# An attention kernel on one core: each output projection's seven products put into one run, its reads due first, and all dates of the build-time planner replaced

## The chip, the cores and the metric

The kernel runs on one core of a Trainium2 chip. The metric is the time of one execution in device microseconds; the median of three runs of the kernel before is 1901.77 us (1901.64 to 1901.78). Names of engines: PE is TensorE's matmuls and PEld its loads of weights, DVE is VectorE, ACT ScalarE, POOL GpSimd, SP the queue of SyncE that issues most transfers.

## The reference

A cross-attention layer with a residual, followed by a linear state-space scan over the same rows and a few small outputs. Cut to the attention, which is nearly all of the work (T = 4096 queries, S2 = 3202 keys, H = 512, 8 heads of 64, fp32):

```python
q, k, v = heads(q_in, Wq, bq), heads(kv_in, Wk, bk), heads(kv_in, Wv, bv)
scores = einsum('bhqd,bhkd->bhqk', q, k) / sqrt(HD)
out = einsum('bhqk,bhkd->bhqd', softmax(scores), v)
x1 = x + out @ W_o.T + b_o          # then the scan, state by state, over the rows of x1
```

q_in and kv_in are layer-normed rows of x and of the context.

## The kernel before

**Stages.** A lead (to 196 us) normalises the context and makes keys and values. The main loop (196.1 to 1846.3 us) goes over 8 blocks Q of 512 queries, in each over 4 pairs of heads and 2 halves of the queries: 64 units. A unit has 13 chunks of keys, and for each chunk: a score group s on TensorE (L1133, 16 records of 64x64 tiles in the trace), its exponential p on ScalarE (L1211), the product with the values po on TensorE (L1269, 16 records), and the addition of p to a running sum acc on VectorE (L1219). The last chunk is a half one. At a unit's end acc is folded (L1226), swapped and gathered (L1238, L1243), summed by a matmul pd (L1298), inverted (L1342 and L1347), joined (L1320 and L1324) and scaled (L1358). A tail (1846.3 us to the end) finishes the last block's output projection (yb, L2076), the state-space scan (a chain of small steps z over PE, ACT and DVE, L1924 to L1966), its products py and pd_last (L1998) and the joins of the rows (L2012 to L2018), and a short chain of its own for the last rows (zl, py_o1, xr_l: L2115 to L2225).

**Two modes of the array.** Score and value products use TensorE as four tiles of 64x64 (in the planner "quarters"); projections use the full 128x128 array. Here an interruption means a stretch of full-array work inside the stream of quarters.

**Projections by seven products.** A block's queries and its outputs are projected as 2x2 blocks with seven products in place of eight. `project_by_sevenths` makes the output projection of the blocks 0 to 6 (block 7 has `project`). Its pieces: `load` and `row` bring the rows of x and add the bias (SP and POOL); four sums `so` on VectorE ("5": a21 + a22 into a spare tile, "6": that minus a11, "7": a11 - a21 in place, "3": a12 minus sum 6); seven products in the order of CHAIN, 1 2 6 5 7 3 4, of eight records and 128x256 each; and after each one a read on VectorE that adds the accumulator to x1. The weights of the products are W_o or sums of its parts (`to`, made by POOL at L1508). Two accumulators alternate: pax for 1, 6, 7, 4, pay for 2, 5, 3. Products 1 and 2 add to nothing before them; 6 follows 1 in pax once read 1 is done, 5 follows 2 in pay after read 2, 7 after read 6, 3 after read 5, 4 after read 7. Sum 5 waits for product 1, since the tiles of o that the sums use are taken up by `open_left`, which product 1 calls; so the sums cannot be made ahead of the first product.

**Who sets the order.** All instructions are ordered at build time by the class `Plan`, a list scheduler: each piece has an engine, a cost, the pieces it waits for, rings of buffers it takes and gives, and a due date. At each step an engine takes the ready piece that fits and has the earliest due date. SHIFT adds to the due date of each sort of piece a number of steps (one step is about one chunk). A full-array piece gets a date earlier by KEEP while the array is already full, and later by ALONE if no other full-array piece is ready; ENTER and LEAVE are planning costs of a change of mode. `PORT` lists VectorE's pieces that the planner does not put beside GpSimd's. The resulting order of each engine is fixed in the program; at run time the semaphores decide when each instruction starts.

The seven products get their place by this (`at` is the place in CHAIN):

```python
plan.add((*key, k), "PE", 1740, partial(product_, k), after + last_scale,
         d + STEP * 3 // 4 + at - (plan.ALONE if at > 1 else 0),
         ["m", "m"] if k == "1" else [], gives[k])
plan.add(("outs.read", Q, k), "DVE", 690, partial(read, k), [(*key, k)], d + at,
```

The functions that the change touches:

## Time and profile before

| what | us |
| --- | --- |
| median of 3 runs | 1901.77 (1901.64 to 1901.78) |
| the profiled execution, and its span | 1901.72, 1899.8 |
| lead / main loop / tail | 0 to 196.0 / 196.0 to 1846.3 / 1846.3 to 1899.8 |
| busy PE, DVE, ACT, POOL | 1884.8, 1545.2, 1178.1, 253.5 |
| granted clock of TensorE | 0.998 |

The 1.9 us between the profiled execution and its span lie ahead of the first and behind the last instruction. The page's chain of the work that ended last is empty for this trace, so the reading goes by the busy time of stretches, by the groups of instructions and by the timeline: its rows give start, duration, engine, line, operation, out<-in, tile, shape and count, and in brackets the idle time before and who ended it. The ends of matmuls are modelled: their pace is to be taken from start to start. A busy TensorE in the main loop does not mean that it loses nothing: what a change of mode costs lies inside the busy time. Block 0's output projection starts at 430.54 us and block 1's at 637.62; the queries of block 2 are projected at 546.16.

### The profile page before, as it was taken

The numbers are of one execution on the slowest core, as the hardware profiler recorded it, in microseconds if no ns is written. First come the engines' busy times: TensorE is split into PE (matmuls) and PEld (weight loads), VectorE is DVE, ScalarE is ACT, GpSimd is POOL, SyncE is SP. The second block draws the span as 40 slices with busy tenths as digits, with TensorE's granted clock in tenths as the row PEclk, the third lists the DMA queues.
The fourth block names the chain that finished last, engine by engine and source line by source line (L and its number), as shares of the span: only waits on it lengthen the run. The fifth ranks groups of instructions, "written<-read, shape, count | busy, mean of one in ns | idle before, by whom it ended". The sixth has DMA issues, their size and how long they took to land.

```text
span 1899.8 us, 68757 instructions
## 1 busy us (share of the span) xinstructions
PE 1884.8 (99%) x29632; PEld 1383.5 (73%) x29632; DVE 1545.2 (81%) x2114; ACT 1178.1 (62%) x1677; POOL 253.5 (13%) x386
## 2 busy tenths in 40 slices
PE   9999999999999999999999999999999999999997
PEld 5887678777777777777777777777777777777684
DVE  6642699788978898799978897889969997988776
ACT  3242677575767567666766576657766675657653
POOL 6120300022000310022002200021002200120105
PEclk9999999999999999999999999999999999999999
DMA  8654233133323343223413332324312331536476
GB/s 254 159 158 118 59 103 91 41 112 91 97 74 105 92 110 89 77 76 105 112 43 113 83 110 78 105 78 113 101 55 89 112 104 44 171 111 177 136 200 225
DMA packets 260768, 207.55 MB, mean 109 GB/s; under 512 B 94632, under 2 KB 233896, under 8 KB 260460
## 3 DMA queue, kind: packets, MB, share of 16 engines
q1 hardware_dynamic: 256440, 196.48, 36.3%
q10 hardware_dynamic: 4020, 6.62, 1.2%
q8 instruction: 235, 3.85, 0.9%
q14 instruction: 73, 0.60, 0.1%
HBM read 156.32 MB, written 29.88 MB: 98 GB/s over the span
## 4 chain that ended last, share of the span: by engine, by line


## 5 line engine op out<-in xcount | busy, mean ns | idle before, releaser
L1211 ACT ACTIVATE p<-s,shifts 128x1024 f32<-128x1024 f32 (+1 forms) x832 | 895.0, 1082 | 458.1 <-PE s L1133 441.4
L1219 DVE TENSOR_TENSOR acc<-p,acc 128x1024 f32<-128x1024 f32 (+1 forms) x704 | 838.1, 1191 | 107.8 <-ACT p L1211 82.9
L1269 PE MATMUL po<-p,v 64*64 64x256 f32 x12800 | 849.5, 377 | 0.9 <-DVE o L1324 0.9
L1133 PE MATMUL s<-q,k 64*64 64x256 f32 x12800 | 850.1, 377 | 0.3 <-ACT p L1211 0.2
L1133 PEld LDWEIGHTS s<-q,k 64*64 64x64 f32 x12800 | 505.0, 133 | 197.2 <-ACT p L1211 12.9
L1269 PEld LDWEIGHTS po<-p,v 64*64 64x64 f32 x12800 | 504.0, 133 | 172.1 <-issue 6.9
L1622 POOL TENSOR_TENSOR xr<-xr,rowb 128x512 f32<-128x512 f32 x28 | 35.4, 1275 | 842.5 <-DVE acc L1219 842.5
L1347 DVE RECIPROCAL rd<-rd 128x256 f32<-128x256 f32 (+1 forms) x64 | 110.1, 1720 | 9.7 <-ACT rd L1342 9.7
L1219 DVE TENSOR_TENSOR acc<-p,p 128x1024 f32<-128x1024 f32 x64 | 78.1, 1220 | 26.5 <-ACT p L1211 26.4
L1713 POOL TENSOR_TENSOR xr<-x,modb 128x512 f32<-128x512 f32 x28 | 35.5, 1277 | 197.5 <-DVE acc L1219 155.5
L1243 DVE TENSOR_TENSOR acc<-swap,acc 64x256 f32<-64x256 f32 x126 | 56.1, 446 | 1.8 <-ACT swap L1238 0.2
L1204 DVE TENSOR_TENSOR acc<-x,acc 2x256 f32<-2x256 f32 x128 | 54.9, 429 | 1.4
L1409 POOL TENSOR_SCALAR rstd_x<-mv_x 128x1 f32<-128x1 f32 x28 | 18.9, 677 | 269.7 <-DVE mv_x L1406 268.0
L1559 ACT ACTIVATE q<-qx,bias 128x256 f32<-128x256 f32 x42 | 17.6, 471 | 56.8 <-PE qx L393 56.8
L1238 ACT COPY swap<-acc 64x256 f32<-64x256 f32 x126 | 50.9, 404 | 3.0
L571 DVE TENSOR_TENSOR ks<-pky,ks 128x512 f32<-128x512 f32 x15 | 10.4, 692 | 42.9 <-PE pky L393 28.1
L565 ACT ACTIVATE ks<-pkx,bias 128x256 f32<-128x256 f32 x40 | 16.8, 471 | 42.7 <-PE pkx L393 31.2
L1226 DVE TENSOR_TENSOR acc<-acc 128x512 f32<-128x512 f32 x63 | 42.9, 682 | 0.4
L1324 DVE TENSOR_TENSOR o<-po,o 128x256 f32<-128x256 f32 x64 | 26.9, 421 | 8.8 <-ACT o L1320 8.7
L1342 ACT ACTIVATE rd<-pd 128x128 f32<-128x128 f32 x126 | 33.6, 276 | 0.1
L1417 ACT ACTIVATE xh_y<-x,nm_y,rstd_y 128x512 f32<-128x512 f32 x30 | 24.3, 808 | 13.1 <-POOL nm_y L1411 13.1
L1167 DVE TENSOR_REDUCE m<-sm 128x1 f32<-128x256 f32 x64 | 23.8, 413 | 10.1 <-PE sm L1153 10.1
(312 smaller groups left out, 1754.2 us busy)
## 6 DMA issues: line engine op xcount, KB each, us to landing
k<-kd SPq DMA_DIRECT2D x432, 128.0 KB, 2.3
v<-vd SPq DMA_DIRECT2D x432, 128.0 KB, 2.3
xn<-x SPq DMA_DIRECT2D x448, 32.0 KB, 1.9
xr<-in_x_dram SPq DMA_DIRECT2D x30, 256.0 KB, 3.8
x1d<-xr SPq DMA_DIRECT2D x30, 256.0 KB, 2.8
x<-in_x_dram SPq DMA_DIRECT2D x28, 256.0 KB, 3.0
cx<-in_ctx_dram SPq DMA_DIRECT2D x25, 256.0 KB, 5.0
kd<-ks SPq DMA_DIRECT2D x20, 256.0 KB, 2.3
```

The costliest lines, as they stand in the source:

```text
L1133: nc.tensor.matmul(s[k0 : k0 + HD, a, b, :], kts[(*w["at"][:2], c)][r, b * CK + k0 : b * CK + k0 + HD], q[r], start=True, stop=True, skip_ ...
L1204: made = nc.vector.tensor_tensor(to[r], t[r], to[r], ALU.add)
L1211: nc.scalar.activation(t[:, :, :nb, :], w["ps"][c][:, :, :nb, :], AF.Exp, bias=w["shift"])
L1219: return nc.vector.tensor_tensor(w["acc"][:, :, :nb, :], t[:, :, :nb, :], before[:, :, :nb, :], ALU.add)
L1226: return nc.vector.tensor_tensor(acc[:, :, 0, :], acc[:, :, 0, :], acc[:, :, 1, :], ALU.add)
L1238: nc.scalar.copy(w["swap"][r], of[(1 - k) * HD : (2 - k) * HD])
L1243: made = nc.vector.tensor_tensor(of[r], w["swap"][r], of[r], ALU.add)
L1269: nc.tensor.matmul(w["po"][k][a * HD : (a + 1) * HD, :QU], vts[Q, hp, c][r, b, a * HD : (a + 1) * HD], t[r, a, b, :], start=(c == 0 and b ...
L1342: nc.scalar.activation(to, of, AF.Copy, accum_out=rises[:, 3 * i + k : 3 * i + k + 1])
L1347: nc.vector.reciprocal(w["rd"][:, part], (w["pd"] if last else w["rd"])[:, part])
L1622: return nc.gpsimd.tensor_tensor(xs[half][:, t], xs[half][:, t], rowb, ALU.add)
L1713: return nc.gpsimd.tensor_tensor(xt[:, t], x1[:, t], modb, ALU.add)
```

## The change

Three things change in the code.

1. *Seven products in one run.* `open_left` may be called by sum 5 as well, so sum 5 no longer waits for product 1; and product 1 now waits for the sums 6 and 7.
2. *Reads first, and room for them.* The reads of both chains, outputs and queries, get due dates earlier by ALONE (30 us). The planner notes when each read of these chains will be ready; `fits` refuses a piece on the same engine, VectorE or ScalarE, that would start before that and end over WAITS (600 ns) after it.
3. *New dates.* SHIFT is replaced as a whole (two of its lines are shown); 22 sorts that had no entry have one.

```diff
+    KEEP, ALONE, WAITS = 6000, 30000, 600
+    CHAINS = "outs", "sevenths"
-        "row.store": -0.5, "fold": 17, "rows.outs": 10.5, "heads": -12, "spread": 1.75, "query.flip": -11,
...
+        "row.store": 2.25, "fold": 21, "rows.outs": -27.25, "heads": 29.5, "spread": 4.5, "query.flip": -21,
...
-        last, now, port, before, events, out = None, 0, 0, None, [], []
+        last, now, port, before, reads, events, out = None, 0, 0, None, dict(DVE=[], ACT=[]), [], []
...
         def fits(p):
...
+            if any(now < r < now + p["cost"] - self.WAITS for r in reads.get(p["engine"], [])[-2:]):
+                return False
...
                     last = p["kind"]
+                    if p["name"][0] in self.CHAINS:
+                        on = pieces[(p["name"][0] + ".read", *p["name"][1:])]["engine"]
+                        reads[on].append(now + cost + self.LATE[e])
...
-            plan.add(("sevenths.read", Q, k), on, 850 if on == "ACT" else 690, partial(read, k), [(*key, k)], d + at, [], gives)
+            plan.add(("sevenths.read", Q, k), on, 850 if on == "ACT" else 690, partial(read, k), [(*key, k)],
+                     d + at - plan.ALONE, [], gives)
...
         def open_left():
+            if left:
+                return
...
             if k == "5":
+                open_left()
...
-            after = {"5": scales(*a21) + scales(*a22) + [(*key, "1")], "6": [("so", Q, "5")],
+            after = {"5": scales(*a21) + scales(*a22), "6": [("so", Q, "5")],
...
-            "1": scales(*a11) + [("to", "4")] + [(*k, "row") for ks in kss for k in ks],
+            "1": scales(*a11) + [("to", "4")] + [("so", Q, k) for k in "67"]
+            + [(*k, "row") for ks in kss for k in ks],
...
-            plan.add(("outs.read", Q, k), "DVE", 690, partial(read, k), [(*key, k)], d + at,
+            plan.add(("outs.read", Q, k), "DVE", 690, partial(read, k), [(*key, k)], d + at - plan.ALONE,
```

No instruction is added or removed: the same matmuls, operations and transfers stand in another order. In the names below the first number of s, po, p and acc is the block whose heads are worked on, then the pair of heads, the half and the chunk.

TensorE at block 1's output projection, before: the middle one of its three interruptions, with products 5, 6, 3 and 7. Products 1 and 2 stand one score group earlier (ahead of the product with chunk 6), product 4 alone behind that with chunk 8.

```order
L1133 MATMUL s_2_0_1_11_7775<-q_2_0_6561,k_2_0_0_11_7156 64x256 x8
L393 MATMUL pay_1_7735<-to5_2260,so_1_7756 128x256 x4
L393 MATMUL pax_1_7734<-to5_2260,so_1_7756 128x256 x4
L393 MATMUL pay_1_7735<-wo_97,o_1_2_0_6209 128x256 x4
L393 MATMUL pax_1_7734<-to7_2316,o_1_0_1_5181 128x256 x4
L1269 MATMUL po0_2_0_1_7585<-p_2_0_1_7_7664,v_2_0_0_7_7158 64x256
```

The same place in the changed kernel:

```order
L1280 MATMUL po1_2_0_1_7579<-p_2_0_1_9_7729,v_2_0_0_9_7212 64x256
L404 MATMUL pax_1_7820<-wo_97,o_1_0_0_4720 128x256 x4
L404 MATMUL pay_1_7821<-wo_97,o_1_2_0_6202 128x256 x4
L404 MATMUL pax_1_7820<-to5_2277,so_1_7765 128x256 x4
L404 MATMUL pay_1_7821<-to5_2277,so_1_7765 128x256 x4
L404 MATMUL pax_1_7820<-to7_2337,o_1_0_1_5177 128x256 x4
L404 MATMUL pay_1_7821<-wo_97,o_1_2_0_6202 128x256 x4
L404 MATMUL pax_1_7820<-to7_2337,o_1_2_1_6565 128x256 x4
L1144 MATMUL s_2_1_0_1_7893<-q_2_0_6586,k_2_1_0_1_7541 64x256 x8
```

The seven stand together, in CHAIN's order, behind the value product of chunk 9 and the first score group of the next unit: some three chunks later than the first product stood. Blocks 0 to 5 look alike; block 6's seven are together as well.

VectorE at the same place, before (from read 1; x1_512 and x1_768 are the two halves of the rows, so_1 and o_1 what the sums write):

```order
L1667 TENSOR_TENSOR x1_512_7754<-pax_1_7734,xr_512_7182 128x2x256
L1649 TENSOR_TENSOR so_1_7756<-o_1_0_1_5181,o_1_2_1_6567 128x512
L1667 TENSOR_TENSOR x1_512_7754<-pay_1_7735,x1_512_7754 128x2x256
L1649 TENSOR_TENSOR so_1_7756<-so_1_7756,o_1_0_0_4721 128x512
L1649 TENSOR_TENSOR o_1_0_1_5181<-o_1_0_0_4721,o_1_0_1_5181 128x512
L1649 TENSOR_TENSOR o_1_2_0_6209<-o_1_2_0_6209,so_1_7756 128x512
L1219 TENSOR_TENSOR acc_2_0_1_7530<-p_2_0_1_8_7688,acc_2_0_1_7530 128x1024
L1667 TENSOR_TENSOR x1_768_7798<-pay_1_7735,xr_768_7214 128x2x256
```

And in the changed kernel:

```order
L1230 TENSOR_TENSOR acc_2_0_1_7529<-p_2_0_1_9_7729,acc_2_0_1_7529 128x1024
L1682 TENSOR_TENSOR x1_512_7837<-pax_1_7820,xr_512_7180 128x2x256
L1230 TENSOR_TENSOR acc_2_0_1_7529<-p_2_0_1_10_7740,acc_2_0_1_7529 128x1024
L1682 TENSOR_TENSOR x1_512_7837<-pay_1_7821,x1_512_7837 128x2x256
L1664 TENSOR_TENSOR o_1_2_0_6202<-o_1_2_0_6202,so_1_7765 128x512
L1682 TENSOR_TENSOR x1_512_7837<-pax_1_7820,xr_512_7180 128x2x256
L1230 TENSOR_TENSOR acc_2_0_1_7529<-p_2_0_1_11_7772,acc_2_0_1_7529 128x1024
L1682 TENSOR_TENSOR x1_768_7864<-pay_1_7821,xr_768_7235 128x2x256
L1230 TENSOR_TENSOR acc_2_0_1_7529<-p_2_0_1_12_7792,acc_2_0_1_7529 128x2x256
L1237 TENSOR_TENSOR acc_2_0_1_7529<-acc_2_0_1_7529 128x2x256
L1682 TENSOR_TENSOR x1_768_7864<-pax_1_7820,x1_768_7864 128x2x256
L1682 TENSOR_TENSOR x1_512_7837<-pay_1_7821,x1_512_7837 128x2x256
```

Sums 5, 6 and 7 have gone ahead of read 1, with the adds of chunks 7 and 8 and two gathers among them; the reads of a run follow with an add or sum 3 in between. Read 4 comes after another gather and one row's statistics.

In the tail, TensorE ahead of the third step z of the scan behind the loop, before (xn_l and xh_yl belong to the last rows):

```order
L1998 MATMUL py_o0_24446<-c2_21297,scan_21301 64x256
L2125 MATMUL pu_l0_24468<-xn_l_24418,wc_85 64x128 x4
L2115 MATMUL py_o1_24447<-ident_65,xh_yl1_24459 128x128 x4
L1924 MATMUL z_24397<-scan_21301,a_t_91 64x128 x2
L1998 MATMUL py_n_24448<-c2_21297,scan_21301 64x256
```

And now:

```order
L2014 MATMUL py_o0_24446<-c2_21296,scan_21300 64x256
L2131 MATMUL py_o1_24447<-ident_65,xh_yl1_24459 128x128 x4
L2141 MATMUL pu_l0_24475<-xn_l_24418,wc_85 64x128 x4
L2141 MATMUL py_o1_24447<-xn_l_24418,wc_85 64x128 x4
L1940 MATMUL z_24382<-scan_21300,a_t_91 64x128 x2
L2014 MATMUL py_n_24448<-c2_21296,scan_21300 64x256
```

The last rows' inputs (the second group on py_o1) have come ahead of that step from behind the next one, and the terms zl made from them stand behind the step, where they stood four steps later. The group pd_last of the loop's last unit now stands ahead of all groups yb, where it stood between them.

More of the change, by code (lines that the diff above doesn't have):

```diff
@@ L99 @@
-        "close": -10, "swap": -2.25, "products": -9, "gather.l": -4, "l.ys": -10, "fall.l": -2.5,
-        "weights": -3.5, "rows.s": 2, "l.x1": 1, "l.kept": 6, "tq": 20, "l.store": 10, "row.move3": 11,
-        "l.from": -5, "l.copy": -12, "l.states": -8, "l.turn": 4, "row.flip": 3.75, "swap.l": -18, "l.near": 4,
-        "differ": 12.25, "row.load": 12, "add": -6, "rest.l": -8, "den.l": 11.5, "query.factors": 16,
-        "sevenths": -6, "l.z": 1, "scale.l": -0.5, "outs": -3, "output": -12, "query.move3": 3, "number": 0.25,
@@ new lines @@
+        "fall.l": -46.25, "weights": -14, "rows.s": -6.5, "l.x1": 12.25, "l.kept": 1.5, "tq": 37.5,
+        "l.store": 35, "row.move3": -73, "l.from": 2.5, "l.copy": -22.75, "l.states": -42.5, "l.turn": -27.25,
+        "row.flip": -51, "swap.l": -30.75, "l.near": -25.75, "differ": 2.25, "row.load": 38, "add": 3.25,
+        "rest.l": -23, "den.l": -33, "query.factors": 32, "sevenths": 5, "l.z": -5.75, "scale.l": 64.25,
+        "outs": 1.5, "output": -59, "query.move3": 10, "number": -8.75, "l.inputs": -15, "q": -3.75,
@@ L109 @@
+        "row.x1": 30.75, "join.l": 99.75, "start": 18.5, "sevenths.read": -15.75, "product": 0.5,
+        "row.factors": -40, "fold.l": 20, "output.l": 47, "table": -34.75, "gather": 18, "outs.read": -15,
+        "copied": 0.5, "open": -6.25, "row.copy": 48.5, "l.out": 31.75, "l.factors": -10.25, "a": 32.5,
+        "query.move1": 5.25, "fetch": 19.75, "py1": 22.75,
     }
```

20 lines of the change are left out of this document (10 added, 10 removed).

## The prediction

> **What bounds the kernel now.** I read the busy time by stretch first, then the groups by line, then TensorE's and VectorE's timeline around one block's output projection, and last the rows that end the program.
>
> ```profile
> 196.00:1846.30 1650.30, 1648.56 (x28250) 1210.01 (x28246) 1416.73 (x1850) 1094.82 (x1502) 176.22 (x242) 1.00 0.35 98
> 1846.30:1899.80 53.50, 42.59 (x520) 25.58 (x512) 33.42 (x82) 15.98 (x54) 24.71 (x31) 0.95 0.73 231
> L1269 PE MATMUL po<-p,v 64*64 64x256 f32 x12800 | 849.5, 377 | 0.9 <-DVE o L1324 0.9
> L1133 PE MATMUL s<-q,k 64*64 64x256 f32 x12800 | 850.1, 377 | 0.3 <-ACT p L1211 0.2
> ```
>
> The first two rows give, for the main loop and for the tail, the length and then the busy time of PE, PEld, DVE, ACT and POOL, the granted clock, and what the DMAs moved. In the loop TensorE is busy for 1648.56 of 1650.30 us, and the two large groups waited for other engines for 0.9 and 0.3 us in all. So the loop is as long as TensorE's list of work, and only three things can shorten it: fewer interruptions of the list, fewer stalls, or a shorter tail. No matmul goes. The tail is different: TensorE has 11 us free there, and a chain over several engines sets its end.
>
> How much an interruption costs is to be read from the starts of the groups (the modelled ends overlap). Block 1:
>
> ```profile
> 634.73 1.24 PE L1133 MATMUL s<-q,k 64*64 64x256 f32 x16
> 635.59 1.24 PE L1269 MATMUL po<-p,v 64*64 64x256 f32 x16
> 636.46 1.24 PE L1133 MATMUL s<-q,k 64*64 64x256 f32 x16
> 637.62 1.99 PE L393 MATMUL pax<-wo,o 128*128 128x256 f32 x8
> 639.45 1.89 PE L393 MATMUL pay<-wo,o 128*128 128x256 f32 x8
> 641.27 1.09 PE L1269 MATMUL po<-p,v 64*64 64x256 f32 x16
> 642.19 1.04 PE L1133 MATMUL s<-q,k 64*64 64x256 f32 x16
> 643.16 1.99 PE L393 MATMUL pay<-to,so 128*128 128x256 f32 x8
> 644.99 1.89 PE L393 MATMUL pax<-to,so 128*128 128x256 f32 x8
> 646.72 1.89 PE L393 MATMUL pay<-wo,o 128*128 128x256 f32 x8
> 648.44 1.89 PE L393 MATMUL pax<-to,o 128*128 128x256 f32 x8
> 650.26 1.09 PE L1269 MATMUL po<-p,v 64*64 64x256 f32 x16
> 651.18 0.61 PE L1133 MATMUL s<-q,k 64*64 64x256 f32 x8
> 651.61 1.04 PE L1269 MATMUL po<-p,v 64*64 64x256 f32 x16
> 652.58 1.99 PE L393 MATMUL pax<-to,o 128*128 128x256 f32 x8
> 654.51 1.09 PE L1133 MATMUL s<-q,k 64*64 64x256 f32 x16
> ```
>
> Undisturbed, 16 records take 0.865 us from start to start (634.73, 635.59, 636.46), and a product inside a run 1.725 (644.99, 646.72, 648.44). From 636.46 to 654.51 stand five groups of 16, one of 8 and seven products: 5 x 0.865 + 0.43 + 7 x 1.725 = 16.83 us of work in 18.05 us. The 1.22 us of difference are three interruptions, and 0.19 that the first entry has beyond the others: 636.46 to 637.62 is 1.16 us, 642.19 to 643.16 only 0.97. That leaves 0.34 for each, with a little slow start after the last one still to come. The queries' products, which already are one run, say the same:
>
> ```profile
> 545.62 0.61 PE L1269 MATMUL po<-p,v 64*64 64x256 f32 x8
> 546.16 1.99 PE L393 MATMUL qx<-xn,wq 128*128 128x256 f32 x8
> ...
> 559.36 1.04 PE L1269 MATMUL po<-p,v 64*64 64x256 f32 x16
> ```
>
> Left out are the other six products and one full group. From 545.62 to 559.36 is 13.74 us for 0.43 + 7 x 1.725 + 0.865 = 13.37 of work: one interruption, **0.36 us**, and its entry (0.54 after a half group of 0.43) has no extra 0.19.
>
> **The change, term by term**, against the profiled execution (1901.72 us, 0.05 below the median; 1.9 of it outside the span).
>
> *Interruptions.* Blocks 0 to 6 go from three to one each, block 7 stays as it was: 14 x 0.36 = **-5.0 us** (-4.8 at 0.34). This depends on nothing but the order.
>
> *First entries.* In the new order the first product stands behind a po group, as the queries' first does, not behind an s group as at 636.46. If that removes the 0.19: 7 x 0.19 = **-1.3 us**; if it belongs to the product itself, 0. The queries' entry is the nearest row, so I take it, and keep 0 for the range.
>
> *The reads.* What was free is now near the path: a run of seven has two banks, and its third product must find the first read, on VectorE, done. Rows of VectorE around the same place (start, duration), and the group of the gathers:
>
> ```profile
> 637.93 1.30 DVE L470 STREAM_TRANSPOSE x<-xh_x 128x512 f32<-128x512 f32 x2 [1.01 <-ACT xh_x L1417]
> ...
> 645.87 1.22 DVE L1219 TENSOR_TENSOR acc<-p,acc 128x1024 f32<-128x1024 f32 x1
> 647.00 0.68 DVE L1667 TENSOR_TENSOR x<-pax,xr 128x512 f32<-128x512 f32 x1
> 647.60 1.22 DVE L1219 TENSOR_TENSOR acc<-p,acc 128x1024 f32<-128x1024 f32 x1
> ```
>
> ```profile
> L1243 DVE TENSOR_TENSOR acc<-swap,acc 64x256 f32<-64x256 f32 x126 | 56.1, 446 | 1.8 <-ACT swap L1238 0.2
> ```
>
> From start to start an add takes 1.13 (645.87 to 647.00) and a read 0.60 (647.00 to 647.60), together 1.73, the pace of a product; a sum, of the same shape, I take to be as long as a read. A product can be read 2.0 us after its start (644.99 to 647.00). In the new order of block 1 the run starts 5.6 us of TensorE work later than before, at 637.6 + 5.6 = 643.2 on the old clock. Until read 1 VectorE does, from 637.93 on, two transposes (1.23), three sums (1.8), adds 7, 8 and 9 (3.4) and the two gathers (0.9), so it is free at 645.3, and read 1 is due at 645.2. The third product starts at 643.2 + 3.55 = 646.8 and read 1 ends at 645.9: 0.9 us of slack. Then add 10 and read 2 (ready 646.9, done 647.6, wanted 648.5), sum 3, read 6 (ready 648.7, done 649.4, wanted 650.2), add 11 and read 5 (done 651.1, wanted 651.9), half add, fold, read 7 (done 652.9, wanted 653.7). Each has about 0.8 us left, so the run costs **0**; the same pattern repeats for blocks 0 to 5. The sums of the first product (the last one ends by 641.4) are ready 1.8 us before it. ScalarE gets only two scores to work on in the run, and four groups of p lie in stock when it ends.
>
> *The rest of the loop.* All dates are new, so small stalls go and come. One large one is in the first unit of block 0:
>
> ```profile
> 225.52 2.95 DVE L1204 TENSOR_TENSOR acc<-x,acc 2x256 f32<-2x256 f32 x2
> 228.97 1.74 PE L1269 MATMUL po<-p,v 64*64 64x256 f32 x27 [0.92 <-DVE o L1324]
> ```
>
> VectorE needs 2.95 us for two tiny adds, and TensorE idles 0.92 for the copy of po behind them. Now a score group (0.865) of the next chunk stands ahead of that po and fills the hole: **-0.9**, or 0 if it only moves. Small waits elsewhere in the loop make up the rest of its 1.7 us without PE work. New ones cannot be read from the trace: from 0 to +6 (0.9, the one above, in each of seven blocks). Nearest is what the old order has, a total near 1.7; I take **+1.0**.
>
> *Tail.* The rows that end it:
>
> ```profile
> 1860.47 0.66 PE L2115 MATMUL py_o<-ident,xh_yl 128*128 128x128 f32 x4
> 1862.93 1.09 PE L2125 MATMUL py_o<-xn_l,wc 128*64 128x128 f32 x8
> 1868.64 1.04 PE L1924 MATMUL zl<-scan,a_t 64*64 64x128 f32 x16
> 1889.77 0.28 PE L1924 MATMUL py_o<-scan,c 64*64 64x32 f32 x4
> 1890.71 0.69 DVE L2018 SCALAR_TENSOR_TENSOR row<-pd_last,row 128x512 f32<-128x512 f32 x1 [1.12 <-ACT y_l L2012]
> 1891.31 0.86 DVE L2171 SCALAR_TENSOR_TENSOR scan<-scan 128x128 f32<-128x128 f32 x1
> 1894.27 0.68 DVE L2221 SCALAR_TENSOR_TENSOR xr_l<-py_o,xr_l 128x512 f32<-128x512 f32 x1
> ```
>
> The last rows' own short chain starts at 1868.64 and ends last, at 1894.9, behind the join of the last row block at 1890.71. In the new order its inputs (the rows at 1860.47 and 1862.93) stand ahead of the third z step and its terms behind that step, some 5 us sooner; its states are done before the long chain is, and its two products follow that chain's last one directly. Its end then is the join (1890.71 + 0.60) and two reads of 0.60: 1892.5, 2.4 us sooner. Against that, 1.09 us now stands ahead of a z step. I take -2.4 + 0.9 = **-1.5**, from -4 (the long chain loses nothing, and the pd_last group that now precedes all of yb saves a change of shape and its wait) to +1.5 (both moved groups, 0.66 and 1.09, delay the long chain and the store of the last rows stays where it is).
>
> Sum: -5.0 - 1.3 - 0.9 + 1.0 - 1.5 = -7.7, and 1901.7 - 7.7 = **1894.0 us**.
>
> **Rivals.** *VectorE paces the run (ends on the other side).* If VectorE comes to read 1 with one reciprocal (1.75 by the row below) and one add (1.22) more than I listed, read 1 is 2.97 late, of which 0.9 is slack; TensorE waits 2.1 us in each run, 7 x 2.1 = 14.7, and the time is 1908.7. It decides from 0.9 us of lateness on, and the whole gain is gone from 0.9 + 1.1 = 2.0.
>
> ```profile
> 632.31 1.75 DVE L1347 RECIPROCAL rd<-rd 128x256 f32<-128x256 f32 x1
> ```
>
> For it: VectorE is busy for 1417 of 1650 us and all seven reads are its own. Against: in the new order of block 1 one reciprocal comes ahead of the sums and the next behind read 4, and in the run's 12.3 us it has 8.2 of work up to read 7. Chance 0.09. The Trainium skill, "TensorEngine Tiling (Array Packing)", section PSUM Bottleneck, advises to empty the accumulators with both ScalarE and VectorE; by that rule this run, with ScalarE idle and VectorE on every read, is the wrong one. The rows above (0.60 of a read against 1.73 of a product) do not bear that out for this run, hence the small chance.
>
> *ScalarE is behind after the run.* It has little to do in the run; if VectorE's backlog (the statistics of the rows and the reciprocal) holds p tiles back, TensorE could idle 0.9 per block as at 228.97: +6.3, or 1900.3. For it: the copies of the joins lie behind these. Against: four groups of p in stock, and the old four-product run at 643.16 left no gap behind. Chance 0.10.
>
> *The tail gives back.* The long chain is delayed by both moved groups, +1.5 in place of -1.5: 1897.0. Chance 0.17; still faster.
>
> *Entries and stalls stay as they are* (no -1.3, no -0.9, +1.0 and tail 0): 1901.7 - 5.0 + 1.0 = 1897.7, the border. Chance 0.12. That the products do not come together at all is excluded by the order.
>
> **How the numbers follow.** The forecast's own case has 0.52. About 0.2%, 3.8 us, is what a measurement of this kernel can tell from no change: below 1897.97 is faster. Forecast and tail rival lie there (0.69), the fourth case to nearly three quarters (0.08): 0.77. Within: the rest of it and the ScalarE case, 0.14. Slower 0.09. The range goes down to -5.0 - 1.3 - 0.9 + 0 - 4 = -11.2 (1890.5, and a little for the unlisted), up to the ScalarE rival's lower part; the slower rival and part of ScalarE's are left out: 1890.0 to 1900.0.
>
> **What would show it.** Right: in each of blocks 0 to 6 one run of seven products that lasts 12.2 to 12.4 us from its first start to the next group's, entered 0.97 to 1.0 us after a full group, with no wait for VectorE at its products; no idle 0.92 near 229; last read of the last rows near 1886. Wrong: products more than 1.83 apart inside a run, TensorE's groups L1269 or L1133 with several us of idle time for ACT or DVE, or a tail over 54 us.

## The result, and the profile after

The changed kernel takes **1893.65 us** (median of 6 runs, 1892.99 to 1896.34) against 1901.72 us of the kernel before on the same chip (6 runs, 1901.18 to 1902.16): a ratio of 0.9959, interval 0.9947 to 0.9972. That is 8.1 us less; 1894.0 was forecast. The interval lies below 1, so the gain is clear of the noise, small as it is. The profiled execution was the longest of the six (1896.34); the same kernel was profiled a second time (run again, 1893.54), and both profiles are shown.

Busy time by stretch, first the changed kernel: main loop, tail, and twelve microseconds at the loop's end. The columns are length, then busy time of PE, PEld, DVE, ACT and POOL, granted clock, DMA share, GB/s.

```profile
195.91:1840.35 1644.44, 1640.96 (x28256) 1226.69 (x28248) 1423.90 (x1854) 1091.80 (x1502) 180.35 (x242) 1.00 0.35 98
1840.35:1894.50 54.15, 41.76 (x507) 24.78 (x502) 33.24 (x77) 16.00 (x54) 24.46 (x31) 0.93 0.77 228
1828.00:1840.00 12.00, 10.14 (x186) 8.73 (x181) 9.41 (x13) 6.18 (x11) 0.00 (x0) 1.00 1.06 225
```

The second profile of the same kernel:

```profile
195.87:1837.45 1641.58, 1639.97 (x28255) 1227.22 (x28248) 1423.43 (x1854) 1091.83 (x1502) 180.32 (x242) 1.00 0.35 99
1837.45:1891.80 54.35, 41.76 (x510) 24.77 (x502) 33.35 (x78) 16.01 (x54) 24.46 (x31) 0.94 0.68 223
1828.00:1840.00 12.00, 12.00 (x202) 10.54 (x195) 10.79 (x16) 6.50 (x12) 0.00 (x0) 1.00 1.05 292
```

Before, the loop took 1650.52 us from the first score group to the last value product (196.14 to 1846.66) and the tail 53.14. So the loop is **8.9 us** shorter and the tail **1.2** longer (second profile; 6.1 and 1.0 in the first, whose 2.86 us more in the loop are the matter of the first experiment). PE's busy time in the loop fell from 1648.78 (196.14 to 1846.66) to 1639.97, by 8.8, with no matmul less: interruptions count as busy.

TensorE around block 1's projection, second profile (start, duration, engine, line, operation, out<-in, tile, shape, count):

```profile
640.37 1.04 PE L1280 MATMUL po<-p,v 64*64 64x256 f32 x16
641.35 1.99 PE L404 MATMUL pax<-wo,o 128*128 128x256 f32 x8
643.18 1.89 PE L404 MATMUL pay<-wo,o 128*128 128x256 f32 x8
...
651.81 1.89 PE L404 MATMUL pax<-to,o 128*128 128x256 f32 x8
653.63 1.09 PE L1144 MATMUL s<-q,k 64*64 64x256 f32 x16
...
655.41 0.40 PE L1309 MATMUL pd<-acc,ones 64*64 64x128 f32 x8
655.62 1.04 PE L1144 MATMUL s<-q,k 64*64 64x256 f32 x16
```

Seven products (four are left out; inside the run each starts 1.73 after the one ahead) without a gap: 641.35 to 653.63 is 12.28 us, the entry 0.98 (640.37 to 641.35), and no row waits. The other six runs have the same 12.28 and an entry (from the start of the full group ahead to the first product) of 0.97 to 0.98, but for block 6's of 1.06.

VectorE's reads beside it (first profile, whose rows stand 0.04 us later here):

```profile
643.49 0.69 DVE L1682 TENSOR_TENSOR x<-pax,xr 128x512 f32<-128x512 f32 x1
...
646.88 0.69 DVE L1682 TENSOR_TENSOR x<-pax,xr 128x512 f32<-128x512 f32 x1 [0.36 <-PE pax L404]
```

Between the two stand an add, the second read and a sum. The third read waits for its product, not the product for the read: VectorE is ahead. What else became shorter is seen in the groups. Of before, the denominators' matmuls pd; of the second profile, the values' group and the same one:

```profile
L1298 PE MATMUL pd<-acc,ones 64*64 64x128 f32 x504 | 29.0, 272 | 0.2
```

```profile
L1280 PE MATMUL po<-p,v 64*64 64x256 f32 x12800 | 840.7, 376 | 0.9 <-DVE o L1335 0.9
L1309 PE MATMUL pd<-acc,ones 64*64 64x128 f32 x504 | 26.9, 272 | 0.0
```

The values' records cover 8.8 us less than before (849.5), the interruptions and long entries among them. 504 pd records have the same mean, yet cover 2.1 us less, and no column of idle time shows where they came from. The rows of before do:

```profile
628.91 1.04 PE L1133 MATMUL s<-q,k 64*64 64x256 f32 x16
629.98 0.70 PE L1298 MATMUL pd<-acc,ones 64*64 64x128 f32 x5
...
631.28 1.24 PE L1133 MATMUL s<-q,k 64*64 64x256 f32 x16
```

```profile
629.01 0.86 DVE L1243 TENSOR_TENSOR acc<-swap,acc 64x256 f32<-64x256 f32 x2
```

A full group of s takes 0.865 us, but pd starts 1.07 after 628.91: the second gather on VectorE ends at 629.87, and pd, which reads what it gathers, starts behind it. 0.21 us are lost there. From 629.98 to 631.28 are 1.30 us for pd (0.22, as in 655.41 to 655.62 above) and one value group (0.865): 0.21 more, so **0.42** in each of blocks 0 to 5. In the second profile above, pd (655.41) stands behind gathers that ended at 653.48, and from 655.41 to 655.62 there is no gap. The idle time shows almost nothing of it since the modelled ends (1.04 for a group that the next one follows after 0.87) cover the hole.

The same wait has a second cost, which the durations show. The group ahead of pd is 1.04 us long, the one at 631.28 is 1.24, and so are those up to the first product at 637.62. In a group of 1.04 us the records start by fours, within 0.02 us, as four tiles work side by side; in one of 1.24 the first record starts 0.20 ahead of the next three. I read this as one of the tiles being that much ahead of the others; the starts of the groups, still 0.865 apart, are then its own. The next full-array product pays for it: the entry behind a group of 1.24 is 1.16 (636.46 to 637.62), behind one of 1.04 it is 0.97 (642.19 to 643.16). This holds throughout: of 419 entries into a product or a pu group behind a full group, in the loops of all fourteen traces, 418 cost 0.10 us plus the lead of that first record, within 0.02 (with 0.05 more where the group itself stands right behind full-array work). The second group of the matmuls pu (128x64 tiles, an interruption too) had a lead of 0.10 before and has none now:

```profile
528.78 1.14 PE L1269 MATMUL po<-p,v 64*64 64x256 f32 x16
529.86 1.09 PE L1729 MATMUL pu<-xn,wc 128*64 128x128 f32 x16
```

```profile
527.54 1.04 PE L1280 MATMUL po<-p,v 64*64 64x256 f32 x16
528.51 1.09 PE L1745 MATMUL pu<-xn,wc 128*64 128x128 f32 x16
```

**Where the loop's 8.9 us came from**: 14 interruptions of 0.365 = 5.1 (a full group's 0.865 becomes an entry of 0.97, first and last product are 0.1 longer each, 0.05 behind the last); the wait of pd, 6 x 0.42 = 2.5, and the first entries that it made 0.19 longer in the same six blocks, 1.1 (block 6 had no such wait and no such entry); the entry into the second pu group, 1.07 before and 0.97 now in six blocks, 0.6. A new hole of 0.08 behind two score groups, at seven places, takes back 0.6. These come to 8.7, against 8.9.

The Trainium skill, "TensorEngine Tiling (Array Packing)", section Key Properties, says that changing the tiling mode drains TensorE. The trace agrees in so far as each stretch of full-array work costs TensorE time, and gives the price that the page does not state: 0.365 us.

### The profile page after: what moved, and what is told of

Same layout as the page of the kernel before. It is cut to its first block, busy times and chain, and to the rows that moved or that the text cites. A ratio compares the mean times of both kernels' runs of the same rounds, so it can differ in the third digit from the quotient of the medians.

```text
span 1894.5 us, 68673 instructions
## 1 busy us (share of the span) xinstructions
PE 1876.3 (99%) x29632; PEld 1399.4 (74%) x29632; DVE 1552.2 (82%) x2114; ACT 1175.2 (62%) x1677; POOL 257.3 (14%) x386
## 4 chain that ended last, share of the span: by engine, by line
PE 97%; DVE 1%; ACT 1%; issue 0%; DMA 0%; POOL 0%; SPq 0%; DVEq 0%; ACTq 0%
PE po L1280 36%; PE s L1144 36%; PE qx L404 3%; PE pax L404 3%; PE pay L404 2%; PE qy L404 2%; PE pkx L404 2%; PE pvx L404 2%; PE pvy L404 1%; PE pky L404 1%; PE pk L722 1%; PE pv L599 1%; PE pd L1309 1%; PE pu L1745 1%; PE sm L1164 1%; PE po L1268 1%
## 5 line engine op out<-in xcount | busy, mean ns | idle before, releaser
L1230 DVE TENSOR_TENSOR acc<-p,acc 128x1024 f32<-128x1024 f32 (+1 forms) x704 | 849.2, 1213 | 103.2 <-ACT p L1222 82.0
L1280 PEld LDWEIGHTS po<-p,v 64*64 64x64 f32 x12800 | 509.6, 133 | 173.6 <-issue 6.4
L1729 POOL TENSOR_TENSOR xr<-x,modb 128x512 f32<-128x512 f32 x28 | 41.6, 1497 | 253.8 <-DVE acc L1254 178.8
L1237 DVE TENSOR_TENSOR acc<-acc 128x512 f32<-128x512 f32 x63 | 43.1, 685 | 0.5
L481 DVE STREAM_TRANSPOSE x<-xh_y 128x512 f32<-128x512 f32 x28 | 18.2, 688 | 22.1 <-ACT xh_y L1428 12.5
```

Of the source, the lines that this page charges most:

```text
L1230: return nc.vector.tensor_tensor(w["acc"][:, :, :nb, :], t[:, :, :nb, :], before[:, :, :nb, :], ALU.add)
L1237: return nc.vector.tensor_tensor(acc[:, :, 0, :], acc[:, :, 0, :], acc[:, :, 1, :], ALU.add)
L1280: nc.tensor.matmul(w["po"][k][a * HD : (a + 1) * HD, :QU], vts[Q, hp, c][r, b, a * HD : (a + 1) * HD], t[r, a, b, :], start=(c == 0 and b ...
L1729: return nc.gpsimd.tensor_tensor(xt[:, t], x1[:, t], modb, ALU.add)
```

## The experiments

Each run was made beside runs of the kernel before on the same chip (medians 1901.46 to 1901.75). Ratios are to these.

**1. The changed kernel once more (again).** No edit. The question was whether two waits at the loop's end, in the first profile, belong to the order. They cost 0.69 us at the first of these rows and 1.95 at the second:

```profile
1829.94 0.37 PE L1280 MATMUL po<-p,v 64*64 64x256 f32 x1 [0.27 <-issue]
...
1838.56 1.29 PE L1280 MATMUL po<-p,v 64*64 64x256 f32 x18 [1.58 <-issue]
```

> The changed kernel unchanged, for a second look and a second set of times. Theory A: the two waits of TensorE in the last unit (0.7 us at 1830.1 and 1.95 us at 1838.6 in the profile after, put down to issue) are late loads of its instructions behind the burst of row loads, so they are not part of the order and change from execution to execution: times between 1893 and 1896.5, and the profile shows these two waits with other lengths, while the shorter gaps of the loop (0.55 near 1793.6, 1.09 near 228.8) are the same to 0.02. Rival B: they belong to the order (a semaphore that the trace doesn't show): both are there again at the same places within 0.1 us.

Measured: 1893.54 (1893.31 to 1895.49; ratio 0.9960, 0.9946 to 0.9974). Neither wait is there: PE is busy for all of the 12 us in which it was busy for 10.14 in the first profile. What differs is the transfer that runs there, 32 loads of rows on the SP queue, first profile and second:

```profile
1818.79 30.46 SPq L1901 DMA_DIRECT2D row<-x1d  x32
```

```profile
1818.73 24.77 SPq L1901 DMA_DIRECT2D row<-x1d  x32
```

The same 32 loads took 30.46 us in the one and 24.77 in the other (all DMAs together moved 225 and 292 GB/s from 1828 to 1840). Over all fourteen traces such waits of TensorE are there in the six in which the loads took 28.2 us or more (0.4 to 2.65 us in all) and absent in seven of the eight with 27.8 or less; read1_x4, with 26.95, has one of 0.4. So they are not part of the order, and 2.65 of the 2.86 us by which the first profile's loop is longer are these.

What TensorE waits for there can be narrowed down by counting. In every trace that has such a wait, it stands where 58,561 or 58,817 profiled instructions of TensorE's queue (matmuls, weight loads, semaphores) lie ahead: the two places are 256 instructions apart, and they are the same in reads_plain, whose order ahead of them is another. So the place goes with the count of instructions, and not with the tile or the semaphore that is next. That fits instructions which are brought in by blocks of 256 and come late beside the burst. No run shows this loading itself, and why the transfers differ from run to run stays open.

**2. One value product put back into each run (split).** This undoes the change's core in blocks 0 to 6, two products and five, and leaves all dates.

```diff
+        made, pieces = {}, plan.order()
+        for Q in range(NQB - 1):
+            a, b = [next(i for i, p in enumerate(pieces) if p["name"] == ("outs", Q, k)) for k in "26"]
+            c = next(i for i, p in enumerate(pieces) if p["name"] == ("outs", Q, "4"))
+            s = next(i for i in range(c, len(pieces)) if pieces[i]["name"][0] == "product")
+            pieces.insert(b, pieces.pop(s))
```

> Each run of seven products in blocks 0 to 6 is split in two and five by one value product (the chunk product that stands behind the run is put between its second and third product); nothing else moves. Theory A: an interruption of the four-tile stream costs about 0.36 us wherever it stands: 7 x 0.36 = 2.5 us more than the changed kernel, 1896.2 against 1893.65. Rival B: the gain came from the other moves (statistics, sums, gathers) and an interruption itself costs under 0.1: 1893.6 to 1894.3.

Measured: 1900.77 (1899.88 to 1902.08; ratio 0.9996, 0.9987 to 1.0006), 7.2 us above the run again. TensorE and VectorE in block 1:

```profile
644.15 1.89 PE L404 MATMUL pay<-wo,o 128*128 128x256 f32 x8
...
648.83 1.89 PE L404 MATMUL pay<-to,so 128*128 128x256 f32 x8
...
655.83 1.09 PE L1144 MATMUL s<-q,k 64*64 64x256 f32 x16
657.25 0.45 PE L1309 MATMUL pd<-acc,ones 64*64 64x128 f32 x8 [0.33 <-DVE x L1682]
```

```profile
656.54 0.66 DVE L1682 TENSOR_TENSOR x<-pax,xr 128x512 f32<-128x512 f32 x1
```

The interruption itself costs what was said: from 644.15 to 648.83, a product, the po group and a product, are 4.68 us for 2 x 1.725 + 0.865 = 4.315 of work: **0.365**. But a block is 0.91 us longer, not 0.36. The rest is a wait that the edit made: the po group was taken from between s and pd, and pd now needs the bank of PSUM that the last read (656.54 + 0.66) frees; 655.83 to 657.25 is 1.42, 0.5 of it lost beyond the group of s and its 0.05 of slow start. That it is the bank is read from the code, where pd takes its banks from the ring of the products, and from the releaser in the row, which is this read. So the expected total was missed by a side effect, while its term was confirmed.

**3 and 4. The first read done twice, and four times (read1_x2, read1_x4).** How much slack has the third product, and is it VectorE that it would wait for? Repeats of read 1 add the accumulator again, so x1 is wrong by that; nothing else changes.

```diff
-            nc.vector.tensor_tensor(t, of, xs[m][:, :, cs] if k in "1654" else t, ALU.add)
+            for _ in range(4 if k == "1" else 1):
+                nc.vector.tensor_tensor(t, of, xs[m][:, :, cs] if k in "1654" else t, ALU.add)
```

> In each of the seven runs the first read is made twice on VectorE (the second writes the same values), 0.60 us more ahead of everything behind it. Theory A (the prediction's): each read has about 0.8 us of slack against the product that waits for it, so nothing happens: within 0.5 us of the changed kernel. Rival B: VectorE is the pace of the run: 7 x 0.6 = +4.2 us, about 1897.8.

> The first read of each run is made four times, 1.80 us more on VectorE. Theory A (slack 0.8 to 0.9 us): TensorE waits 0.9 to 1.0 us in each run, +6.3 to +7.0, about 1900.3, and the trace has products in the run that start 2.6 to 2.7 us after the one before. Rival B (no slack): 7 x 1.8 = +12.6, about 1906.2. Rival C (the slack is larger, over 1.8): no change.

Measured: twice 1894.84 (1893.57 to 1895.24; ratio 0.9963, 0.9949 to 0.9977), four times 1905.57 (1905.06 to 1906.82; ratio 1.0023, 1.0013 to 1.0032). With four, block 1, TensorE and then VectorE:

```profile
644.96 1.89 PE L404 MATMUL pay<-wo,o 128*128 128x256 f32 x8
648.15 1.99 PE L404 MATMUL pax<-to,so 128*128 128x256 f32 x8 [1.30 <-DVE x L1683]
```

```profile
645.23 2.87 DVE L1683 TENSOR_TENSOR x<-pax,xr 128x512 f32<-128x512 f32 x4
```

Three repeats add 2.18 us (2.87 against 0.69) and the third product comes 3.19 us after the second instead of 1.73, 1.46 later: **0.72 us** of slack. One repeat adds 0.73, and in blocks 0 to 5 the run grows by 0.13 to 0.19 (12.41 to 12.47): 0.01 to 0.10 at the third product and 0.1 at the fourth. So the slack is 0.63 (block 0) to 0.72, not 0.9. Beyond it each late microsecond of VectorE costs one on TensorE: from one repeat to three VectorE has 1.45 us more to do, and block 1's run grows from 12.41 to 13.86, by 1.45. Block 6 has less room: its run is 12.91 with one repeat and 14.36 with three, since products further back wait too. The rival in which VectorE paces the run has its mechanism shown; it is only not reached.

**5. All old dates with the new code (old_dates).** The tables of due dates of before, in the changed kernel.

```diff
-        "row.store": 2.25, "fold": 21, "rows.outs": -27.25, "heads": 29.5, "spread": 4.5, "query.flip": -21,
+        "row.store": -0.5, "fold": 17, "rows.outs": 10.5, "heads": -12, "spread": 1.75, "query.flip": -11,
...
```

> The changed code with the table of dates of before: the seven products of blocks 0 to 5 stand in one run (block 6's in two), reads are due first, but no date is searched. Theory A (the runs make the gain in the loop): the loop gains its 13 interruptions, 4.7 us, but the tail loses (its order shows the last unit's sums behind steps of the scan): loop 4 to 5 shorter than before, tail longer, in all 1898 to 1902. Rival B (the dates make most of it): the loop is no more than 2 us shorter and shows new waits of 5 us or more for VectorE at the products or for ScalarE behind the runs; 1903 or above.

Measured: 1898.03 (1896.43 to 1900.21; ratio 0.9981, 0.9972 to 0.9990). Blocks 0 to 5 have the run of seven (12.28 us, no waits), block 6 five and two. TensorE in block 1:

```profile
628.33 1.04 PE L1139 MATMUL s<-q,k 64*64 64x256 f32 x16
629.40 0.70 PE L1304 MATMUL pd<-acc,ones 64*64 64x128 f32 x5
...
642.57 1.24 PE L1139 MATMUL s<-q,k 64*64 64x256 f32 x16
643.74 1.99 PE L399 MATMUL pax<-wo,o 128*128 128x256 f32 x8
```

pd comes 1.07 us behind the start of s, the groups from there on are 1.24 long, and the run's first product (643.74) comes 1.17 behind the s group ahead of it (642.57): the wait of before is still there, with both of its costs. The loop is 1644.83 us, 5.7 below before and 3.25 above the run again. Of the 5.7, 13 interruptions less make 4.7, and the pu entries, not long here, 0.6. The new dates make most of the other 3.3: the wait of pd (2.5) and the first entries (1.1) go, and the new holes (0.6) come. In the tail the new dates give 0.9 more (55.24 here, 54.35 in the run again). This run keeps the reads' earlier dates and the guard, so it does not show the seven products alone.

**6. The reads without their earlier dates and without the guard (reads_plain).** In both chains' reads:

```diff
-            if any(now < r < now + p["cost"] - self.WAITS for r in reads.get(p["engine"], [])[-2:]):
-                return False
...
-                     d + at - plan.ALONE, [], gives)
+                     d + at, [], gives)
...
-            plan.add(("outs.read", Q, k), "DVE", 690, partial(read, k), [(*key, k)], d + at - plan.ALONE,
+            plan.add(("outs.read", Q, k), "DVE", 690, partial(read, k), [(*key, k)], d + at,
```

> The changed kernel without its second part: the reads keep their ordinary due dates and the planner doesn't keep VectorE and ScalarE clear for them; the seven products still stand in one run and the dates are the new ones. Reads come about one add later on VectorE. Theory A (each read has 0.6 to 0.7 us of slack, and an add ahead of it takes 1.13): TensorE waits inside the runs, 0.4 to 1 us in each output run and as much in the queries' runs, together 4 to 10 us: 1897.5 to 1903.5. Rival B (the reads have room enough): within 1 us of 1893.6.

Measured: 1898.72 (1898.13 to 1900.11; ratio 0.9984, 0.9975 to 0.9993), 5.1 above the changed kernel; but the wait inside the output runs, theory A's mechanism, is not what cost it. The output runs are 12.28 to 12.35 us long. What broke is the queries' run:

```profile
552.78 1.09 PE L1278 MATMUL po<-p,v 64*64 64x256 f32 x16
553.81 1.99 PE L402 MATMUL qy<-tq,sq 128*128 128x256 f32 x8
```

The planner, which now sees the reads late, puts a po group between the third and the fourth product: one interruption (0.36) more. A wait of s for ScalarE elsewhere in the block takes 0.33 and the entry into pu 0.11; a block is 1.0 us longer in all, of which 0.2 was not traced. The profiled execution, the longest of this run (1900.11), has besides these a wait of 1.4 us of the kind of run 1, and its tail is 1.5 us shorter than in the run again, for a reason that was not traced. The reads' dates and the guard keep the queries together; they do little for the outputs. Which of the two does it was not tested.

**7. GpSimd's sums for the weights 36 planner steps later (sums_later).** The stall at 228.97 of before was forecast to go. It stayed; VectorE, GpSimd and TensorE in the first profile:

```profile
225.27 2.95 DVE L1215 TENSOR_TENSOR acc<-x,acc 2x256 f32<-2x256 f32 x2
226.49 1.46 POOL L1519 TENSOR_TENSOR to<-wo,to 128x512 f32<-128x512 f32 x1
228.74 1.74 PE L1280 MATMUL po<-p,v 64*64 64x256 f32 x27 [0.91 <-DVE o L1335]
```

```diff
-        output_weights(plan, [from_(24 * STEP)], 24 * STEP)
+        output_weights(plan, [from_(60 * STEP)], 60 * STEP)
```

> GpSimd's four sums of W_o's parts are made 36 planner steps (some 77 us) later, nothing else is meant to move. Theory A (VectorE's two tiny adds take 2.95 us near 225 because these sums hold it up, and TensorE's idle 0.91 us at 228.7 comes from it): the gap of 1.09 us goes, and no new one of that size comes up where the sums stand now, in the middle of a unit: 0.8 to 1.1 us less, 1892.5 to 1892.8. Rival B: the gap stays (another cause), or moves with the sums: 1893.6.

Measured: 1895.23 (1893.67 to 1897.15; ratio 0.9962, 0.9949 to 0.9976), no gain. The wait at 228.7 is gone: with no sum on GpSimd beside them, the same two adds take 0.84 us in place of 2.95. A larger wait has come with the sums:

```profile
224.47 0.84 DVE L1215 TENSOR_TENSOR acc<-x,acc 2x256 f32<-2x256 f32 x2
...
290.31 2.29 POOL L1519 TENSOR_TENSOR to<-wo 128x512 f32<-128x512 f32 x1
291.36 2.32 DVE L1230 TENSOR_TENSOR acc<-p,p 128x1024 f32<-128x1024 f32 x1
292.56 2.26 POOL L1519 TENSOR_TENSOR to<-wo,to 128x512 f32<-128x512 f32 x1
297.24 2.37 PE L1280 MATMUL po<-p,v 64*64 64x256 f32 x27 [2.23 <-DVE o L1335]
```

So the cause is shown: GpSimd's sums beside VectorE's adds, at the one place as at the other. The add of 1.22 us takes 2.32, and the rows fit together as turns: the first sum ends at 292.60, the add 1.08 later (293.68), the second sum 1.14 after that (294.82). The Trainium skill, "SBUF — State Buffer", section SBUF: two separate sides, calls the port pair that the two engines share an exclusive lock, held for a whole instruction, for a VectorE operation with two SBUF inputs against a GpSimd one that reads SBUF. The trace agrees: each record here holds the wait for the other in it (and 225.27 + 2.95 = 228.22, 0.27 after the sum at 226.49 ended).

**8 to 11. The tail (tail_moved, tail_end, rows_late; late_and_tail is the first and the third together).** In tail_moved the two moved input groups and the terms go one step of the long chain back, apart from each other:

```diff
...
+        for name, other in (
+            (("l.inputs", 0), ("b", "z", 2)), (("l.kept", 0), ("b", "h", 2)), (("l.inputs", 1), ("b", "z", 3)),
+            (("l.kept", 1), ("b", "h", 3)), ("risen", ("l.kept", 1)), ("l.terms", ("b", "z", 4)),
...
+            behind(name, other)
```

In tail_end the last row block is joined and the last two reads are made ahead of VectorE's comparing steps:

```diff
...
+        for name, other in (
+            (("joined0", 15), "l.ys"), (("copied", 15), ("joined0", 15)), (("l.out", 0), ("copied", 15)),
+            (("l.out", 1), ("l.out", 0)), (("differ", "b", 2), ("l.out", 1)),
+        ):
+            behind(name, other)
```

In rows_late the 32 loads of rows start only behind the last chunk's exponential, past the place of the waits of run 1:

```diff
...
+            if piece["name"] == ("fetch", 0):
+                w = made["weights", len(units) - 1, NDC - 1]
+                tc.add_manual_dep(made[piece["name"]].ins, w.ins.name, mybir.DependencyInfo(
+                    mybir.DependencyClass.Sync, mybir.DependencyReason.SCHED_ONLY), reason="rows late")
```

> The changed kernel with the last rows' inputs moved back behind steps of the long scan chain: the two input groups (1.09 us each) stand behind the third and the fourth step, the terms behind the fifth, and the short chain's steps one place later. Theory A: in the changed kernel these groups delay the third step by some 2 us, and the long chain ends the tail, so this gives back about 1.5: 1892.0. Rival B: the short chain is the bound as before, and this makes it 1 to 2 us later: 1894.5 to 1895.5. Rival C: the tail's end is set by the last outputs' reads and transfers: within 0.4 of 1893.6.

> Only VectorE's last eight pieces are put in another order: the join of the last row block and the two reads of the last rows' output go ahead of the steps that compare the scan's ends. Theory A (what the second look shows: those reads end 5.5 us behind the last scan product because the comparing steps, and a 1.13 us one among them, stand ahead of them, and the last transfer sets the end): the last transfer is issued 2.5 us earlier, the store of row block 15 about 0.7 us, and the kernel ends 0.7 to 2 us sooner, 1891.6 to 1892.9. Rival B (the count of bad values, which ends at the same time as the reads, sets the end): within 0.4 of 1893.6.

> One wait more: the first of the 32 loads of row blocks for the tail waits for ScalarE's last exponential, so that the burst of loads starts near 1835 instead of 1818.8 and TensorE's last unit no longer runs beside it. Theory A (TensorE's instructions come late behind the burst): the waits put down to issue near 1830 and 1838 are gone in every execution, the slow executions near 1895 to 1896 disappear, and the median is 0 to 1 us lower, 1892.8 to 1893.6, unless the tail waits for the rows. Rival B (the waits have another cause): they stay, and the spread stays 1893 to 1896.5. Rival C: the rows come too late for their joins and the tail grows by 3 us or more.

> Both edits, the late burst and the moved inputs. If both theories hold their gains add: 1891.3 to 1892.0, and all executions within 0.8 us. If the rows are late for the joins once the long chain is faster, it is no better than the moved inputs alone.

Measured: tail_moved 1893.93 (1893.67 to 1896.14; ratio 0.9962, 0.9948 to 0.9976), tail_end 1893.50 (1893.06 to 1894.70; ratio 0.9959, 0.9945 to 0.9973), rows_late 1898.38 (1897.17 to 1899.12; ratio 0.9983, 0.9974 to 0.9992), late_and_tail 1898.04 (1897.61 to 1899.05; ratio 0.9982, 0.9973 to 0.9991). The order that these edit, TensorE in the run again:

```profile
1848.59 0.44 PE L1940 MATMUL z<-scan,a_t 64*64 64x128 f32 x4 [0.23 <-DVE scan L1975]
...
1852.39 0.33 PE L1940 MATMUL z<-scan,a_t 64*64 64x128 f32 x2
```

The moved groups (1850.04 to 1852.39) stand between the second and the third step of the long chain, which are 3.80 us apart (before, with one of the two groups there, 3.06: 1858.00 to 1861.06). In tail_moved the distance is 2.03 (1850.76 to 1852.79), and yet the chain's last step comes 38.89 us after the last value product, against 38.91: the next steps, beside which the groups and the short chain now stand, give it back. Two chains share three engines there, and what leaves one gap fills another. And the end itself, VectorE in the run again:

```profile
1882.89 0.69 DVE L2034 SCALAR_TENSOR_TENSOR row<-pd_last,row 128x512 f32<-128x512 f32 x1 [0.16 <-issue]
...
1884.51 1.13 DVE L2063 TENSOR_SCALAR scan<-scan 128x32 f32<-128x32 f32 x1
...
1885.78 0.68 DVE L2237 SCALAR_TENSOR_TENSOR xr_l<-py_o,xr_l 128x512 f32<-128x512 f32 x1
```

From the join at 1882.89 to the last read are 2.89 us, 1.7 of it the steps that compare the scan's states. tail_end takes these away from there:

```profile
1887.14 0.15 DVE L2420 TENSOR_SCALAR nbad<-pd_last 1x1 int32<-1x1 f32 x1 [0.33 <-PE pd_last L2413]
```

The last read is 2.1 us sooner (1883.66), the count of the comparing steps 0.8 later (1887.14; 1886.38 in the run again), and the time is the same. So the last read alone does not set the end. What does, out of the last stores and that count, was not settled: the last ACT transfer is issued 5.3 us ahead of the span's end in the run again and 6.9 in tail_end. In rows_late no wait of the kind of run 1 is there (its loads took 26.75 us, so that alone says little) and the loop is 1641.57 us, but the tail is 59.30; the SP queue:

```profile
1864.49 24.47 SPq L2041 DMA_DIRECT2D out_dram<-row  x31
...
1890.19 1.21 SPq L2041 DMA_DIRECT2D out_dram<-row  x1
```

The loads now run from 1834.96 to 1861.71, and the stores out_dram<-row start behind them, ten microseconds later than in the run again (1854.55). The queue is full to the end: its last store is issued at 1890.19, against 1885.63. So the loads have to start early. late_and_tail, with the loads as late, has a tail of 58.3.

**12. The later sums and the earlier end together (end_and_sums).** The edits of sums_later and tail_end in one kernel.

> The end of the tail in the new order and the later sums together. If both theories hold, 1890.6 to 1892.0, ahead of both kernels; if neither, 1893.6.

Measured: 1896.07 (1894.84 to 1897.22; ratio 0.9970, 0.9959 to 0.9981), 2.4 us above the changed kernel: no gain. None of the kernels tried is measurably faster than it.

## Why the prediction was right, point by point

The total (8.1 us less, 7.7 forecast) is right, and so is its largest term, with its mechanism. That the total is so close is luck: the rest of the loop came out 3.7 us better than forecast, the tail 2.7 and the stall 0.9 worse, and these cancel.

- **Interruptions, forecast -5.0: right.** -5.1, by 14 x 0.365, and the same price in split, where one was put back, and in reads_plain, where the planner put one into the queries.
- **First entries, forecast -1.3: nearly right in size, wrong in the reason.** -1.1 from six blocks. The forecast put the extra 0.19 down to the s group ahead of the first product. It is the lead that the wait of pd left in one tile: the row at 643.16 stands behind an s group too and has 0.97, block 6's first product stood behind s groups without a pd wait and had no extra, and in old_dates, where the wait stays, the long entry stays (1.17). It went since the new dates took the wait of pd away, and not since a po group now stands ahead.
- **Reads, forecast 0 with 0.9 us of slack: right in kind.** No product waits in any of seven runs; the slack is 0.63 to 0.72, since read 1 starts 2.1 us after its product (641.39 to 643.49) and is done after 0.69, where the forecast counted 2.0 and 0.60. The rule on emptying accumulators with two engines, weighed there, was not needed: VectorE alone kept up.
- **The stall at 228.97, forecast -0.9: wrong, 0.** The step that failed is "a score group of the next chunk stands ahead of that po": one did not come ahead of that po, whose copy is late because VectorE waits for GpSimd's sums, which the change left beside it. TensorE's order there is the old one (two score groups, sm, po). Run 7 shows that the gap goes where the sums go.
- **Rest of the loop, forecast +1.0: wrong in sign, -2.7** (pd -2.5, pu -0.6, new holes +0.6, and 0.2 that was not traced). The forecast looked for waits in the column of idle time, where all of the old order's added up to 1.7 us, and so saw none of the 2.5 us that pd waited inside modelled ends. They were to be had by the same start-to-start reading that gave the interruptions' price, a few rows ahead of those quoted (628.91 to 631.28); and the rows quoted from 634.73 to 636.46 have the 1.24 that tells of them.
- **Tail, forecast -1.5: wrong, +1.0 to +1.2.** The rival "the tail gives back" (+1.5) was right here. The short chain did come 2.5 us sooner, as worked out (its last products py_a 43.1 us after the last value product, 45.7 before). But the long chain lost 1.4, not 0.9 (its last step at 38.91 us after the last value product, 37.53 before), and the step "its end then is the join" and two reads of 0.60 left out the comparing steps, 1.7 us of VectorE work between join and last read. The last read at 1885.78 looks like the forecast's "near 1886", but only because the loop ended earlier than forecast; the tail's own sign of error, over 54 us, was there (54.15 and 54.35).
- **Rivals.** VectorE pacing the run: its price is shown by read1_x4 (12 us for 1.46 us of lateness in each run and what follows it), its condition was not met. ScalarE behind the run: not there (waits of s for ScalarE 0.2 us in all, as before).

Loop and tail together: -5.1 - 1.1 - 2.7 + 1.2 = -7.7; with the lead, which is 0.3 shorter, these are the 8.0 between the two profiled spans (1899.8 and 1891.8).

## What to carry to other kernels

Where TensorE's list is the bound, price a change of order from start to start, over the whole period of a block, and not by the idle column: here interruptions of 0.36 us and waits of 0.2 lay inside the modelled ends. Where groups of equal size have unequal durations (1.04 and 1.24 here), one tile is ahead of the others, and the next full-array product pays for it: look for the wait that made it so. When products are put together, measure the slack of the reader behind them (here 0.7 us) by repeating one read; it tells how near the run is to being paced by VectorE. A gain on a shared chain that is not the last thing to end (the short chain here) is worth nothing until what ends last, and what runs on the same engines behind it, has been listed instruction by instruction.

## What the runs showed that was not expected

- A wait of 0.2 us inside a group of pd costs as much again at the next full-array product: it leaves one of the four tiles 0.20 us ahead, and that lead is carried over seven groups before it is paid for.
- The same kernel loses 0 to 2.65 us on TensorE, with nothing but "issue" as the releaser, beside a burst of 32 row loads that takes 24.8 to 30.5 us. The places are the same in every trace, 256 instructions of TensorE's queue apart. The first profile, 2.8 us above the second, is the one with the longest burst.
- GpSimd and VectorE take turns: two additions of 2x256 took 2.95 us, a sum on GpSimd 2.29 instead of 1.31, an add on VectorE 2.32 instead of 1.22.
- Removing one value product from ahead of pd cost 0.5 us per block through a bank of PSUM, more than the interruption that the same edit made (0.365).
